# Mamba scan stage of a four-layer convolution network: side jobs carried from block to block, fixed buffers for them, shorter holds of their PSUM banks, sums copied out a few steps later, a quarter of du times B multiplied by diagonal matmuls

## The chip, the cores and the metric

The kernel runs on one core of a Trainium2 chip. A core has five engines that each execute their own instruction list in order: TensorE (PE in the profile; its weight loads are listed apart as PEld), VectorE (DVE), ScalarE (ACT), GpSimd (POOL) and SyncE (SP), which here only issues DMAs. They wait for one another through semaphores. The metric is the device time of one execution in microseconds. Before the change it is 17602.43 us, the median of three executions (17602.12 to 17605.28).

## The reference, cut to what matters

Four layers follow one another on a batch of 8 images of 256 channels and 32 x 32 pixels: an attention block with a feed-forward part, a second attention block, a quantised bottleneck, and a Mamba layer. The change lies in the Mamba layer alone. It reads each image in four directions (rows or columns first, forward or backward), runs the same Mamba on each sequence of L = 1024 tokens, and adds the four results:

```python
def _selective_scan(u, dt, A, Bm, Cm):          # d = 512 channels, n = 16 states
    def step(h, inp):
        u_t, dt_t, B_t, C_t = inp
        dA = jnp.exp(dt_t[:, :, None] * A)
        h = h * dA + dt_t[:, :, None] * B_t[:, None, :] * u_t[:, :, None]
        y = jnp.einsum('bdn,bn->bd', h, C_t)
        return (h, y)
    ...
def _mamba(u, W_in, conv_w, conv_b, W_x, W_dt, b_dt, A_log, D, W_out):
    x, z = jnp.split(u @ W_in.T, 2, axis=-1)
    x = silu(causal depthwise conv of 4 taps of x)           # cut
    x_dbl = x @ W_x.T
    dt = jax.nn.softplus(x_dbl[..., :16] @ W_dt.T + b_dt)
    Bm, Cm = x_dbl[..., 16:32], x_dbl[..., 32:]
    y = _selective_scan(x, dt, -jnp.exp(A_log), Bm, Cm) + x * D
    return (y * jax.nn.silu(z)) @ W_out.T
```

Everything is float32.

## The kernel before

The first phase computes layers one to three and leaves codes of the images in HBM. The second phase is the Mamba layer. It works through 64 blocks: 8 images x 4 directions x 2 halves of 512 tokens. A block has 64 units: for each of the 16 states s, four chunks c of 128 channels. A unit is one scan of 128 channels x 512 tokens on VectorE. Its parts are recorded in this order, and each engine executes its own instructions in the order in which they are recorded (`tc.manual_schedule()`):

```python
    def scaled(u, t):       # du*B of state s for 128 tokens t: tokens on partitions, 512 channels
        o = dbp.tile([P, DI], F32, name="dbu", tag="dbu")
        src, b = d.duT[h * TH + t], d.bT[:, h * TH + t, s : s + 1]
        if t == TH - 1 and s % 2:
            nc.gpsimd.tensor_scalar(o, src, b, zero, ALU.mult, ALU.add)      # L951
        else:
            nc.scalar.activation(o, src, AF.Identity, scale=b)               # L953
    def turned(u):          # turns four 128x128 pieces of it: channels on partitions
        db = ps_d.tile([P, HALF], F32, name="db", tag="db")
        for t, o in enumerate(units["dbu", u - c]):
            nc.tensor.transpose(db[:, t * P : (t + 1) * P], o[:, c * P : (c + 1) * P], ident)   # L962
    def decay(u):           # exp(dt*A)
        nc.scalar.activation(da, d.dt[c, h], AF.Exp, scale=am[:, a : a + 1])  # L973
    def scan(u):            # h = h*dA + db; then, for two chunks at once, h*C
        nc.vector.tensor_tensor_scan(x[:, ::step], da[:, ::step], db[:, ::step], ..., ALU.mult, ALU.add)  # L985
        if c % 2:
            ...             # in a first half: the last column is kept as the state   (L993)
            nc.gpsimd.tensor_tensor(pair, pair, cb.unsqueeze(1).to_broadcast([P, 2, HALF]), ALU.mult)     # L994
    def summed(u):          # adds h*C over the states in PSUM, turned back to tokens on partitions
        for t in range(TH):
            nc.tensor.matmul(banks[t][:, c * P : (c + 1) * P], lhsT=pair[:, c % 2, t * P : (t + 1) * P],
                             rhs=ident, is_transpose=True, ...)               # L1016
        ...                 # in four units of a block also x*D by a diagonal matmul  (L1024)
        if r == PER - 1 and n % 4 != 1:
            ...             # the four sums are copied out of PSUM (or added to yT)   (L1034-1038)

    for u in range(total):              # total = 64 blocks x 64 units, PER = 64
        n, r = divmod(u, PER)
        if r == LAG:                    # LAG = 4
            must, more = side(n)        # the side jobs that later blocks need
            jobs.add(0, must)
            jobs.add(1, more)
        scan(u)
        turned(u + 2)
        decay(u + AHEAD)                # AHEAD = 5
        ...                             # C rows (DMA), scaled() for two states ahead
        summed(u - LAG)
        jobs.step(0.85, 1)              # one step of the side jobs, with 0.85 matmuls and 1 activation of budget
        if r == PER - 8:
            jobs.drain([0])             # all jobs of the first queue are run to their end here
```

The side jobs prepare the next blocks: the input projection (`inputs`, L686), the 4-tap convolution as diagonal matmuls with silu and x_dbl (`mixed`, L738 to L780), dt and du (`steps`, L795 to L832), and they finish earlier ones (`fold`, `outputs`). Each is a Python generator; every `yield` ends its part in one step. At most four of the first queue run at a time; they share two PSUM banks, two sets of temporaries and two z tiles, which they count. A dt job before:

```python
            nc.scalar.activation(t, ps, AF.Abs)              # ps: its PSUM bank
            nc.scalar.activation(t, t, AF.Exp, scale=-1.0)
            nc.scalar.activation(o, t, AF.Ln, bias=1.0)
            nc.vector.tensor_scalar(u1, t, 1.0, -1.0, ALU.add, ALU.add)     # L810
            ...                                              # two steps later
            nc.gpsimd.tensor_tensor(t, t, u1, ALU.subtract)  # L812
            nc.gpsimd.tensor_tensor(o, o, t, ALU.add)        # L813
            ...                                              # four steps later
            nc.vector.scalar_tensor_tensor(o, ps, 0.0, o, ALU.max, ALU.add) # L815: still needs ps
            ...
            nc.gpsimd.tensor_tensor(u1, o, d.xs[c, h], ALU.mult)            # L818
            jobs.give("bank")
            ...                                              # turned by TensorE (L828), copied to duT (L832)
```

Of the kernel before, what the change touches and what calls it, by code (L numbers as in the profile page):

```python
# [547 lines left out]
class _Jobs:  # L548
# [14 lines left out]
    def take(self, what):  # L563
        while not self.room[what]:
            yield
        self.room[what] -= 1

    def give(self, what):
        self.room[what] += 1

    def step(self, pe, act):
        for k, v in (("pe", pe), ("act", act)):
            self.turns[k] = min(self.turns[k] + v, max(v, 1.0))
        for (wait, run), n in zip(self.queues, (4, 2)):
            while wait and len(run) < n:
                run.append(wait.pop(0))
            for j in list(run):
                try:
                    next(j)
                except StopIteration:  # L580
                    run.remove(j)
# [7 lines left out]
def phase_b(ctx, tc, i, col, ident, codes, out):  # L589
# [11 lines left out]
    dbp = ctx.enter_context(tc.tile_pool(name="db", bufs=2 * TH + 1))  # L601
    dap = ctx.enter_context(tc.tile_pool(name="da", bufs=6))
    hp = ctx.enter_context(tc.tile_pool(name="h", bufs=4))
    cbp = ctx.enter_context(tc.tile_pool(name="cb", bufs=3))
    tp = ctx.enter_context(tc.tile_pool(name="tp", bufs=4))
    zp = ctx.enter_context(tc.tile_pool(name="z", bufs=2))
# [5 lines left out]
    ps_p = ctx.enter_context(tc.tile_pool(name="ps_p", bufs=2, space=PSUM))  # L612
# [35 lines left out]
    jobs = _Jobs(bank=2, tmp=2, z=2)  # L648

    def pp():  # L650
        return ps_p.tile([P, HALF], F32, name="pp", tag="pp")

    def tmp():
        return tp.tile([P, HALF], F32, name="tmp", tag="tmp")

    def ztile():
        return zp.tile([P, HALF], F32, name="z", tag="z")
# [9 lines left out]
    def load_x(b, swap, h, box):  # L667

        cd = cdp.tile([P, CC, N], U8, name="cd", tag="cd")
        nc.sync.dma_start(cd, codes[b].rearrange("k p n -> p k n"))  # L670
        yield from lag(3)
        xf = cdp.tile([P, CC, HALF], F32, name="xf", tag="xf")
        for k in range(CC):
            yield from jobs.turn("act")
            if swap:
                v = cd[:, k].rearrange("p (a b) -> p b a", b=WW)[:, 16 * h : 16 * h + 16]
                nc.scalar.activation(xf[:, k].rearrange("p (a b) -> p a b", b=WW), v, AF.Identity, scale=col("s3"))
            else:
                nc.scalar.activation(xf[:, k], cd[:, k, hs(h)], AF.Identity, scale=col("s3"))
        yield  # L680
        box.append(xf)

    def project(xf, m0, ps):
        for k in range(CC):
            yield from jobs.turn("pe")
            nc.tensor.matmul(ps, lhsT=w_in[:, k, m0 : m0 + P], rhs=xf[:, k], start=(k == 0), stop=(k == CC - 1))  # L686
        yield from lag(2)

    def free():
        yield  # L690
        jobs.give("bank")

    def inputs(b, swap, xi, before=lambda: True):

        for h in range(2):
            box = []

            def first(h=h, box=box):
                while not before():
                    yield  # L700
                yield from load_x(b, swap, h, box)

            yield first()
            for c in range(DC):

                def one(h=h, c=c, box=box):
                    while not box:
                        yield
                    yield from jobs.take("bank")
                    ps = pp()  # L710
                    yield from project(box[0], c * P, ps)
                    if h == 0:
                        t = xip.tile([P, N + 2 * PAD], F32, name="xi", tag="xi")
                        nc.gpsimd.memset(t[:, :PAD], 0.0)
                        nc.gpsimd.memset(t[:, PAD + N :], 0.0)
                        xi[c] = t
                    nc.vector.tensor_copy(xi[c][:, PAD + h * HALF : PAD + (h + 1) * HALF], ps)
                    xi["done"] = xi.get("done", 0) + 1
                    yield from free()

                yield one()


    def mixed(n):
# [5 lines left out]
        def conv(c):  # L730
            while xi.get("done", 0) < 2 * DC:
                yield
            yield from jobs.take("bank")
            ps = pp()
            for k in range(4):
                yield from jobs.turn("pe")
                o = PAD + h * HALF + (PAD - k if d.back else k - PAD)
                nc.tensor.matmul(  # L738
                    ps, lhsT=cvd[:, 4 * c + k, :], rhs=xi[c][:, o : o + HALF], start=(k == 0), stop=(k == 3)
                )  # L740
            yield from lag(2)
            yield from jobs.turn("act")
            t = xsp.tile([P, HALF], F32, name="xs", tag="xs")
            nc.scalar.activation(t, ps, AF.Identity, bias=col("cv_b", c))  # L744
            d.xs[c, h] = t
            done.add(c)
            yield from free()
# [10 lines left out]
        def xdbl():  # L758
# [3 lines left out]
            yield from jobs.take("bank")  # L762
            ps = pp()
# [10 lines left out]
            yield from free()  # L774
            yield from jobs.take("bank")
            pt = pp()
# [4 lines left out]
            yield from free()  # L781
# [3 lines left out]
    def steps(n):  # L785
# [4 lines left out]
        def dt(c):  # L790
            yield from jobs.take("tmp")
            yield from jobs.take("bank")
            ps = pp()
# [8 lines left out]
            t = tmp()  # L802
            nc.scalar.activation(t, ps, AF.Abs)
            yield from jobs.turn("act")
            nc.scalar.activation(t, t, AF.Exp, scale=-1.0)
            yield from jobs.turn("act")
            o = dtp.tile([P, HALF], F32, name="dt", tag="dt")
            nc.scalar.activation(o, t, AF.Ln, bias=1.0)
            u1 = tmp()
            nc.vector.tensor_scalar(u1, t, 1.0, -1.0, ALU.add, ALU.add)  # L810
            yield from lag(2)
            nc.gpsimd.tensor_tensor(t, t, u1, ALU.subtract)  # L812
            nc.gpsimd.tensor_tensor(o, o, t, ALU.add)  # L813
            yield from lag(4)
            nc.vector.scalar_tensor_tensor(o, ps, 0.0, o, ALU.max, ALU.add)  # L815
            d.dt[c, h] = o
            yield from lag(1)
            nc.gpsimd.tensor_tensor(u1, o, d.xs[c, h], ALU.mult)  # L818
            jobs.give("bank")
# [4 lines left out]
            yield from jobs.take("bank")  # L824
            pt = pp()
# [4 lines left out]
            jobs.give("tmp")  # L830
            for t in range(TH):
                nc.vector.tensor_copy(d.duT[h * TH + t][:, c * P : (c + 1) * P], pt[:, t * P : (t + 1) * P])  # L832
            yield from free()
# [4 lines left out]
    def fold(swap, h):  # L838


        def one(c):
            yield from jobs.take("bank")
            ps = pp()
# [9 lines left out]
            yield from free()  # L853
# [3 lines left out]
    def outputs(b, h):  # L857
        box, done = [], set()

        def gate(c):  # L860
            while not box:
                yield
            yield from jobs.take("z")
            yield from jobs.take("bank")
            ps = pp()
            yield from project(box[0], DI + c * P, ps)

            t = ztile()
            nc.vector.tensor_scalar(t, ps, -44.0, None, ALU.max)
            yield from lag(2)  # L870
# [4 lines left out]
            nc.vector.tensor_tensor(t, ps, t, ALU.mult)  # L875
            yield from free()
            y = ys[c][:, hs(h)]
# [3 lines left out]
            jobs.give("z")  # L881

        def o3(cc):
# [3 lines left out]
            yield from jobs.take("z")  # L887
            yield from jobs.take("bank")
            ps = pp()
# [8 lines left out]
            o = ztile()  # L898
            nc.scalar.copy(o, ps)
            nc.sync.dma_start(out[b, cc * P : (cc + 1) * P, hs(h)], o)  # L900
            yield from free()
            jobs.give("z")
# [40 lines left out]
    def scaled(u, t):  # L943

        if u >= total:
            return
        n, d, h, s, _ = at(u)
        o = dbp.tile([P, DI], F32, name="dbu", tag="dbu")
        src, b = d.duT[h * TH + t], d.bT[:, h * TH + t, s : s + 1]
        if t == TH - 1 and s % 2:  # L950
            nc.gpsimd.tensor_scalar(o, src, b, zero, ALU.mult, ALU.add)  # L951
        else:
            nc.scalar.activation(o, src, AF.Identity, scale=b)  # L953
        units.setdefault(("dbu", u), []).append(o)

    def turned(u):
# [4 lines left out]
        for t, o in enumerate(units["dbu", u - c]):  # L961
            nc.tensor.transpose(db[:, t * P : (t + 1) * P], o[:, c * P : (c + 1) * P], ident)  # L962
# [43 lines left out]
    def summed(u):  # L1006
# [23 lines left out]
        if r == PER - 1 and n % 4 != 1:  # L1030
            for t in range(TH):
                o = yT[:, h * TH + t, :]
                if n % 4 == 3:
                    nc.vector.tensor_tensor(o, banks[t], o, ALU.add)  # L1034
                elif t % 2:
                    nc.vector.tensor_copy(o, banks[t])
                else:
                    nc.scalar.copy(o, banks[t])
# [6 lines left out]
    for t in range(TH):  # L1045
        scaled(DC, t)
# [3 lines left out]
    for u in range(total):  # L1050
        n, r = divmod(u, PER)
        if r == LAG:
# [4 lines left out]
        scan(u)  # L1057
        turned(u + 2)
# [3 lines left out]
        if c >= 1:  # L1062
            scaled(u - c + 2 * DC, c - 1)
        if c == DC - 1:
            scaled(u - c + 2 * DC, c)
        summed(u - LAG)
        jobs.step(0.85, 1)
        if r == PER - 8:
            jobs.drain([0])
    for u in range(total, total + LAG):  # L1070
        summed(u - LAG)
    jobs.add(0, fold(True, 0) + outputs(B - 1, 0) + outputs(B - 1, 1))
# [119 lines left out]
```

## Time and profile before

The trace covers one execution of 17602.1 us. The Mamba blocks begin with the first scan at 9475 us and end with the last at 17545 us.

| stretch | us | PE busy | DVE busy | ACT busy | POOL busy |
|---|---|---|---|---|---|
| layers one to three and set-up | 9475 | 8380 | 2362 | 2018 | 486 |
| 64 Mamba blocks | 8070 | 6678 | 5833 | 5985 | 6399 |
| last sums and outputs | 57 | 41 | 18 | 18 | 14 |

A busy share is an average over a stretch with different limits inside. TensorE's ends are modelled, so that a busy PE is not a PE at its peak: matmuls that follow one another overlap in the records, and the distance from start to start tells what one really costs. A float32 matmul stands in the records as two of the same shape, a transpose as one. In the rows of groups the columns are line, engine, operation, output<-inputs, shapes and count; then busy us and mean ns of one; then the idle time of the engine before them with what ended most of it. "issue" there means that no wait was seen to end.

### The profile page before, as it was taken

The numbers are of one execution on the slowest core, as the hardware profiler recorded it, in microseconds if no ns is written. First come the engines' busy times: TensorE is split into PE (matmuls) and PEld (weight loads), VectorE is DVE, ScalarE is ACT, GpSimd is POOL, SyncE is SP. The second block draws the span as 40 slices with busy tenths as digits, with TensorE's granted clock in tenths as the row PEclk, the third lists the DMA queues.
The fourth block names the chain that finished last, engine by engine and source line by source line (L and its number), as shares of the span: only waits on it lengthen the run. The fifth ranks groups of instructions, "written<-read, shape, count | busy, mean of one in ns | idle before, by whom it ended". The sixth has DMA issues, their size and how long they took to land. (4 is left out here: it accounts for less than half of the span.)

```text
span 17602.1 us, 170403 instructions
## 1 busy us (share of the span) xinstructions
PE 15098.7 (86%) x66144; PEld 10332.0 (59%) x66144; DVE 8213.0 (47%) x8852; ACT 8021.1 (46%) x12205; POOL 6899.4 (39%) x4689
## 2 busy tenths in 40 slices
PE   8988988979889889798897888888888888888888
PEld 5655655556556555565564665656666565666666
DVE  3123123131231231312314776767777776777777
ACT  2221222222222222222224777777777777777777
POOL 0001001010010010100104787878787787878778
PEclk6556556565565565655657999999999999999999
DMA  0000000000000000000000111111111111111111
GB/s 15 0 2 3 0 1 3 0 3 0 1 3 0 1 3 0 3 0 1 0 0 23 35 37 37 36 36 37 37 36 37 37 36 37 36 37 36 35 38 38
DMA packets 177335, 319.06 MB, mean 18 GB/s; under 512 B 20417, under 2 KB 37185, under 8 KB 176530
## 3 DMA queue, kind: packets, MB, share of 16 engines
q1 hardware_dynamic: 176530, 308.17, 5.7%
q8 instruction: 524, 8.59, 0.2%
q14 instruction: 281, 2.30, 0.0%
HBM read 295.51 MB, written 12.58 MB: 18 GB/s over the span
## 5 line engine op out<-in xcount | busy, mean ns | idle before, releaser
L994 POOL TENSOR_TENSOR h<-h,cb 128x1024 f32<-128x1024 f32 x2048 | 4834.0, 2369 | 945.5 <-issue 407.8
L962 PE MATMUL db<-ident,dbu 128*128 128x128 f32 x16384 | 2769.9, 293 | 895.8 <-DVE h L985 720.0
L973 ACT ACTIVATE da<-dt,am 128x512 f32<-128x512 f32 x4096 | 2899.4, 714 | 911.7 <-DVE h L985 896.6
L305 DVE TENSOR_REDUCE mx<-p 128x1 f32<-128x1024 f32 x768 | 940.6, 1225 | 5034.8 <-PE p L300 5034.8
L314 PEld LDWEIGHTS p<-t,t 128*128 128x128 f32 x12288 | 2576.1, 318 | 1100.9 <-issue 1037.0
L312 ACT COPY t<-pt 128x1024 f32<-128x1024 f32 x768 | 777.2, 1012 | 5102.3 <-PE pt L310 5102.3
L962 PEld LDWEIGHTS db<-ident,dbu 128*128 128x128 f32 x16384 | 2005.8, 149 | 1817.2 <-issue 835.7
L1016 PE MATMUL py<-ident,h 128*128 128x128 f32 x16384 | 2656.0, 288 | 253.0 <-POOL h L994 250.4
L300 PE MATMUL p<-t,t 32*128 32x512 f32 x3072 | 2781.0, 1055 | 0.0
L314 PE MATMUL p<-t,t 128*128 128x32 f32 (+1 forms) x12288 | 2686.0, 398 | 18.0 <-ACT t L312 18.0
L953 ACT ACTIVATE dbu<-duT,bT 128x512 f32<-128x512 f32 x3584 | 2496.9, 710 | 318.2 <-PE db L962 314.3
L985 DVE TENSOR_TENSOR_SCAN h<-da,st,db 128x512 f32<-128x512 f32 x2048 | 2504.6, 1265 | 283.9 <-PE db L962 263.6
L985 DVE TENSOR_TENSOR_SCAN h<-da,db 128x512 f32<-128x512 f32 x2048 | 2385.6, 1205 | 391.0 <-PE db L962 361.0
L1016 PEld LDWEIGHTS py<-ident,h 128*128 128x128 f32 x16384 | 2062.2, 149 | 333.1 <-POOL h L994 329.9
L274 POOL TENSOR_SCALAR t<-t,ga,gs 128x1024 f32<-128x1024 f32 x32 | 37.9, 1195 | 5170.3 <-DVE gs L271 5170.3
L310 PE MATMUL pt<-ident,t 128*128 128x128 f32 x6144 | 1473.6, 418 | 110.5 <-ACT t L307 105.8
L300 PEld LDWEIGHTS p<-t,t 32*128 32x128 f32 x3072 | 839.9, 306 | 956.2 <-issue 938.5
L310 PEld LDWEIGHTS pt<-ident,t 128*128 128x128 f32 x6144 | 1312.6, 241 | 138.6 <-ACT t L307 107.3
L381 POOL TENSOR_TENSOR t<-t,t 128x1024 f32<-128x1024 f32 x16 | 37.1, 2336 | 3143.9 <-ACT t L378 3143.9
L738 PE MATMUL pp<-xi,cvd 128*128 128x512 f32 x2048 | 997.2, 607 | 5.8 <-ACT xs L744 5.4
L307 ACT ACTIVATE t<-p,mx 128x1024 f32<-128x1024 f32 x768 | 860.0, 1120 | 281.2 <-DVE mx L305 281.2
L342 DVE SCALAR_TENSOR_TENSOR t<-t,cols,t 128x961 f32<-128x961 f32 (+1 forms) x512 | 617.0, 1273 | 1.1
(176 smaller groups left out, 11064.8 us busy)
## 6 DMA issues: line engine op xcount, KB each, us to landing
cb<-c_d SPq DMA_DIRECT2D x1024, 256.0 KB, 3.2
cd<-codes SPq DMA_DIRECT2D x48, 256.0 KB, 3.6
t<-in_x_dram SPq DMA_DIRECT2D x8, 1024.0 KB, 5.0
out_dram<-z SPq DMA_DIRECT2D x32, 256.0 KB, 2.0
codes<-cd SPq DMA_DIRECT2D x16, 128.0 KB, 1.7
c_d<-xd SPq DMA_DIRECT2D x64, 32.0 KB, 1.6
w_pi<-in_w_pi_dram SPq DMA_DIRECT2D x1, 1024.0 KB, 8.5
w_in<-in_w_in_dram SPq DMA_DIRECT2D x1, 1024.0 KB, 4.9
```

What stands on the lines that cost most here:

```text
L300: nc.tensor.matmul(s[:, j : j + HALF], lhsT=q(h)[:, t * P : (t + 1) * P], rhs=k(h)[:, j : j + HALF], start=True, stop=True,)
L305: nc.vector.tensor_reduce(mx, s, AX.X, ALU.max, negate=True)
L307: nc.scalar.activation(e, s, AF.Exp, bias=mx, accum_out=rsum[:, h : h + 1])
L310: nc.tensor.transpose(pt[:, j, :], e[:, j * P : (j + 1) * P], ident)
L314: nc.tensor.matmul(po[:, h * hd : (h + 1) * hd], lhsT=et[:, j, :], rhs=vt[:, j, h * hd : (h + 1) * hd], start=(j == 0), stop=(j == NT - 1),)
L738: nc.tensor.matmul(ps, lhsT=cvd[:, 4 * c + k, :], rhs=xi[c][:, o : o + HALF], start=(k == 0), stop=(k == 3))
L953: nc.scalar.activation(o, src, AF.Identity, scale=b)
L962: nc.tensor.transpose(db[:, t * P : (t + 1) * P], o[:, c * P : (c + 1) * P], ident)
L973: nc.scalar.activation(da, d.dt[c, h], AF.Exp, scale=am[:, a : a + 1])
L985: nc.vector.tensor_tensor_scan(x[:, ::step], da[:, ::step], db[:, ::step], 0.0 if first else d.st[:, a : a + 1], ALU.mult, ALU.add)
L994: nc.gpsimd.tensor_tensor(pair, pair, cb.unsqueeze(1).to_broadcast([P, 2, HALF]), ALU.mult)
L1016: nc.tensor.matmul(banks[t][:, c * P : (c + 1) * P], lhsT=pair[:, c % 2, t * P : (t + 1) * P], rhs=ident, is_transpose=True, start=(s == 0 ...
```

## The change

1. Side jobs may be left over. The full drain at unit 56 of every block goes; in its place the recording runs job steps only until the four du tiles of the next block are there. Jobs that are not needed yet go on in the next block. Five jobs of the first queue may run at a time instead of four, and a step has 0.8 matmuls of budget instead of 0.85. In the last two blocks nothing is left to do there.
2. Buffers of side jobs are fixed by number (`pp0`, `pp1`, `tmp0` to `tmp3`, `z0`, `z1`) and handed round in a list. This, with a token for the image tile (`xf`) and a flag that x_dbl is there, keeps jobs of two blocks apart.
3. PSUM banks are held for less time: dt reads its bank with VectorE right after the first exponential and frees it; the gate multiplies y by z straight from PSUM and frees the bank before its three activations.
4. The block's sums are copied out of PSUM one unit later, after the scan of unit 4 of the next block instead of at the end of unit 3.
5. Of the four 128-token pieces of `du*B`, the last is no longer scaled (by GpSimd or ScalarE) and then transposed. GpSimd makes a 128x128 diagonal of B (`dg`), and TensorE multiplies the unscaled duT by it, which scales and turns at once. `da` gets 7 buffers instead of 6, `dbu` 7 instead of 9, `dg` 3.

The number of the other instructions stays. The diff, cut to its core:

```diff
-        for (wait, run), n in zip(self.queues, (4, 2)):
+        for (wait, run), n in zip(self.queues, (5, 2)):
...
-    dbp = ctx.enter_context(tc.tile_pool(name="db", bufs=2 * TH + 1))
-    dap = ctx.enter_context(tc.tile_pool(name="da", bufs=6))
+    dbp = ctx.enter_context(tc.tile_pool(name="db", bufs=2 * TH - 1))
+    dgp = ctx.enter_context(tc.tile_pool(name="dg", bufs=3))
+    dap = ctx.enter_context(tc.tile_pool(name="da", bufs=7))
...
-    jobs = _Jobs(bank=2, tmp=2, z=2)
+    jobs = _Jobs(bank=[0, 1], tmp=[0, 1], z=[0, 1], xf=[0])
...                                   # in steps(), a dt job
+            while "xd" not in d.done[h]:
+                yield
...
-            t = tmp()
+            t, u1 = tmp(2 * kt), tmp(2 * kt + 1)
             nc.scalar.activation(t, ps, AF.Abs)
+            nc.scalar.activation(t, t, AF.Exp, scale=-1.0)
+            yield from lag(1)
+            o = dtp.tile([P, HALF], F32, name="dt", tag="dt")
+            nc.vector.scalar_tensor_tensor(o, ps, 0.0, t, ALU.max, ALU.add)
+            nc.vector.tensor_scalar(u1, t, 1.0, -1.0, ALU.add, ALU.add)
+            yield from free(kb)
+            yield
             yield from jobs.turn("act")
-            nc.scalar.activation(t, t, AF.Exp, scale=-1.0)
-            ...
-            nc.gpsimd.tensor_tensor(t, t, u1, ALU.subtract)
+            nc.scalar.activation(t, t, AF.Ln, bias=1.0)
+            nc.gpsimd.tensor_tensor(o, o, u1, ALU.subtract)
+            yield
             nc.gpsimd.tensor_tensor(o, o, t, ALU.add)
-            yield from lag(4)
-            nc.vector.scalar_tensor_tensor(o, ps, 0.0, o, ALU.max, ALU.add)
...                                   # scaled() and turned()
-        if t == TH - 1 and s % 2:
-            nc.gpsimd.tensor_scalar(o, src, b, zero, ALU.mult, ALU.add)
-        else:
-            nc.scalar.activation(o, src, AF.Identity, scale=b)
+        if t == TH - 1:
+            o = dgp.tile([P, P], F32, name="dg", tag="dg")
+            nc.gpsimd.tensor_scalar(o, ident, b, zero, ALU.mult, ALU.add)
+            units.setdefault(("dbu", u), []).append((src, o))
+            return
+        o = dbp.tile([P, DI], F32, name="dbu", tag="dbu")
+        nc.scalar.activation(o, src, AF.Identity, scale=b)
...
-            nc.tensor.transpose(db[:, t * P : (t + 1) * P], o[:, c * P : (c + 1) * P], ident)
+            nc.tensor.matmul(
+                db[:, t * P : (t + 1) * P], lhsT=o[:, c * P : (c + 1) * P], rhs=m, is_transpose=m is ident,
+                start=True, stop=True,
+            )
...                                   # the loop over units
-        if r == LAG:
+        if r == LAG + 1:
...
         scan(u)
+        if r == LAG:
+            close(n - 1)              # the sums are copied out here
...
-        jobs.step(0.85, 1)
-        if r == PER - 8:
-            jobs.drain([0])
+        jobs.step(0.8, 1)
+        if r == PER - 8 and n + 1 < len(blocks):
+            e, h = blocks[n + 1]
+            while not {("du", c) for c in range(DC)} <= e.done[h]:
+                jobs.step(1, 1)
```

The change is meant to keep the scan running while side jobs are worked off, and to take scaling work from ScalarE.

## The prediction

> **What bounds the kernel now.** I read the page first: busy shares, then the 40 slices, then the costliest groups. The chain of work that ended last is of no help here; its shares add up to some 5% of the span, because it breaks off soon. The slices show two kernels in one. Until slice 22 GpSimd is almost idle and the TensorE clock is granted at 0.5 to 0.6; after it every engine is busy. The change touches only the second part, so I asked for busy time by stretch: layers one to three, the Mamba blocks, the end.
>
> ```profile
> POOL 0001001010010010100104787878787787878778
> PEclk6556556565565565655657999999999999999999
> ...
> 0.00:9475.00 9475.00, 8380.00 (x25592) 5357.41 (x25592) 2362.03 (x2678) 2017.91 (x2715) 485.83 (x166) 0.58 0.01 2
> 9475.00:17545.00 8070.00, 6677.82 (x40450) 4956.15 (x40451) 5832.97 (x6150) 5984.92 (x9461) 6399.18 (x4514) 0.93 0.12 37
> ```
>
> The columns of the last two lines are the stretch, its length, then busy us of PE, PEld, DVE, ACT and POOL, the granted clock, DMA share and GB/s. So 9475 us stay as they are and 8070 us, 126.1 us for each of 64 blocks, are in play. POOL is busy 6399/64 = 100.0 us of a block, DVE 91.1, ACT 93.5. PE's 104.3 is modelled; its own cost comes from start-to-start distances below. No engine is full, so I looked at one block (the 26th, 12645 to 12777 us) on the timelines of DVE and POOL, where unit 56 ends and the drain begins:
>
> ```profile
> 12734.87 2.45 DVE L985 TENSOR_TENSOR_SCAN h<-da,st,db 128x512 f32<-128x512 f32 x2 [0.15 <-PE db L962]
> 12752.91 0.69 DVE L717 COPY xi<-pp 128x512 f32<-128x512 f32 x1 [15.59 <-PE pp L686]
> ...
> 12768.46 8.30 DVE L985 TENSOR_TENSOR_SCAN h<-da,st,db 128x512 f32<-128x512 f32 x7
> ```
>
> ```profile
> 12769.87 9.40 POOL L994 TENSOR_TENSOR h<-h,cb 128x1024 f32<-128x1024 f32 x4 [25.84 <-issue]
> ```
>
> No scan starts for 31 us, while side jobs alone run; then seven scans go at full pace, 1.15 us each. POOL waits 25.8 us, listed as "issue", yet it ends with the first scans after the drain. Over blocks 8 to 55 of the trace (count from 0) the hole between the 57th and 58th scan is 23.4 us, and such a block takes 127.6 us. POOL idles 27.1 us in it: with the hole and the refill after it this is nearly all of its idle time. Outside, POOL is all but full: 22.1 us of its idle time is booked on instructions after the hole, but some 18 of them end within a few us of it. So between drains GpSimd sets the pace, and the drain is what keeps a block 26 us above GpSimd's own work.
>
> The groups that the sums below use, from the page and from POOL's groups in the set-up stretch (9000 to 9475 us):
>
> ```profile
> L994 POOL TENSOR_TENSOR h<-h,cb 128x1024 f32<-128x1024 f32 x2048 | 4834.0, 2369 | 945.5 <-issue 407.8
> L962 PE MATMUL db<-ident,dbu 128*128 128x128 f32 x16384 | 2769.9, 293 | 895.8 <-DVE h L985 720.0
> L1016 PE MATMUL py<-ident,h 128*128 128x128 f32 x16384 | 2656.0, 288 | 253.0 <-POOL h L994 250.4
> L738 PE MATMUL pp<-xi,cvd 128*128 128x512 f32 x2048 | 997.2, 607 | 5.8 <-ACT xs L744 5.4
> ```
>
> ```profile
> L274 POOL TENSOR_SCALAR t<-t,ga,gs 128x1024 f32<-128x1024 f32 x2 | 2.4, 1194 | 613.8 <-DVE gs L271 613.8
> L638 POOL TENSOR_SCALAR dd<-ident,cols 128x128 f32<-128x128 f32 x4 | 2.3, 602 | 0.0
> L951 POOL TENSOR_SCALAR dbu<-duT,bT,zero 128x512 f32<-128x512 f32 x1 | 0.8, 762 | 2.2 <-DVE duT L832 2.2
> ```
>
> L994 alone is 32 x 2.37 = 75.8 us of a block. L962 and L1016 wait for DVE and for POOL: TensorE is not the first bound yet.
>
> **What the Trainium skill says.** "TensorE: Matmul & The Clock Gate" (Terms) gives the transpose mode as four times faster for float32. "FP8 and Floating Point Precision" (TensorE Precision Notes) says that true float32 takes four passes. The trace agrees on the second and not on the first: a float32 matmul of 128 columns (L1024) stands as two records whose starts are 111 ns apart, 222 ns together; a transpose (L962, L1016) is one record, 109 ns from start to start. So transposing is twice as fast, and the measured 109 and 222 are used. "Perfetto Trace Analysis" (Tensor Engine Instruction) says that the profile's end of a matmul is estimated, which is why I use starts: 293 ns "mean" against 109. The same page (Optimization Strategy) reads consistent bubbles on the engine that should be saturated as a hint at too few buffers. Here the repeated bubble on POOL has another cause, the recorded order: side jobs stand between two scans.
>
> **The change part by part.**
>
> *The drain.* I compared the order of instructions of both programs between the 57th and 58th scan of each block. Before, the eight blocks of an image hold 23, 27, 19, 14, 14, 27, 11 and 14 side matmuls of 512 columns there, 149 in all. After, 14, 3, 24, 7, 1, 0, 14 and 1, which is 64. Two of eight blocks keep a long hole (the third, with four of the gates' projections, two whole dt chains and silu; and the seventh), three or four lose it. Scaled by matmuls the mean hole becomes 23.4 x 64/149 = 10.0 us. Estimated by chains (ACT's silu with its two table loads of 1.28 us, dt's path through PE, ACT, DVE, POOL, PE, DVE of some 9 us) I get 11, 3.5, 20, 5, 2, 0.5, 14 and 2, mean 7.3. I take 9. The work that leaves the hole does not vanish: (149 - 64)/8 = 10.6 matmuls of 2 x 0.43 us (L738 and L686 start 429 to 432 ns apart, two records each) = 9.1 us of PE move among the units of each block.
>
> *du times B.* POOL loses 8 x 0.803 = 6.4 us (L951 over all blocks) and gains 16 diagonals. What does one cost? L951 and L274, both of two operations, give (1194 - 762)/512 = 0.84 ns a column, so some 440 ns at 128 columns; L638, of one operation, took 602 at 128. Start to start that is 0.36 to 0.58. I take 0.40: 6.4 us, so POOL stays at 100 us (103 at worst). ACT loses 8 x 0.71 (L953) = 5.7 us. PE turns 64 transposes a block into matmuls: 64 x (222 - 109) = 7.2 us more.
>
> *Where this puts PE.* Its cost before, by starts: L962 and L1016 256 x 0.109 each = 55.8; L738 32 x 0.43 = 13.8; L686 4.8; L795 4.3; L766 3.4; L1024 3.6; the rest 4.7: 90 us of 126. After: 97 us at full clock, as much as POOL. The clock was granted at 0.93 in this part, which asks for 104 us if it stays.
>
> *Shorter holds.* In blocks 8 to 55 DVE waits 3.6 us a block at L815 for POOL (L813). That goes, since the new form needs only ACT. But DVE is not the bound: its scans wait 9.9 us a block for PE (L962) outside the hole, and POOL is full meanwhile. I count nothing for it. The later copy of the sums moves a wait of under 1 us (L1036 and L1034) and costs nothing either. The fixed numbers change no amount of buffers. The same holds for `da` with 7.
>
> *Sum.* A block is POOL's work plus POOL's idle time. Work 100. Idle: 26.1 x 9/23.4 = 10. A third term is what two nearly full engines cost each other, PE at 97 and POOL at 100 with two db banks and four h pairs between them. From nothing in the trace can I work this out; now 13% of the time in the blocks runs at half clock, and PE's extra 16 us between scans (9.1 + 7.2) meet a slack of 18 us of PE waits there. My guess is 6 us. Together 116 us, 10.1 less than 126.1; 64 blocks: 646 us. 17602 - 646 = 16956, put at 16950.
>
> **Rivals.**
>
> *TensorE becomes the bound.* For: 97 us by starts, 104 at the granted clock, and it works in order, so that a side matmul of 0.86 us in front of a db group delays a scan of 1.15 us; 16 us more per block between scans. Against: it idled 17.9 us a block outside the holes, mostly waiting for scans (11.9), and a denser PE may be granted more clock. If it binds at 0.93 with the hole of 9 us counting half: 104 + 4.5 + waits of 12 = 120 to 122 us, 17210 to 17340.
>
> *GpSimd alone binds and the holes close for good.* For: blocks of few side matmuls (fifth, sixth, eighth) leave nothing in the hole. Against: the third keeps 24. It would give 100 + 5 = 105 to 108 us, 16250 to 16450.
>
> *The hole is hidden anyway, and the work only moves.* If units between drains were as full on every engine as GpSimd's share suggests, moving 9 us of PE work and POOL's dt work into them lengthens them by as much as the hole shrinks. For: POOL's 4.1 us in the hole move as well. Against: the other engines have 10 to 35 us to spare a block. It would leave 124 to 127 us, 17450 to 17650. Slower than before it gets only if dg (needed two units after it is recorded, three before) stalls PE at every state: 16 stalls of 1 us would eat the gain, and twice that would turn it.
>
> **Range and chances.** The middle comes from 116 us a block; 110.5 (holes at 7 us, 2 us of mutual waits) gives 16600, and 122 (TensorE) gives 17340. The range 16600 to 17340 should hold 8 in 10. Over 2% faster is below 17250, that is under 120.6 us a block: 0.77. Within 2%: 0.18. Slower: 0.05.
>
> **What would show it.** Right: stretch one unchanged at 9475; holes between 57th and 58th scan of 5 to 12 us, long ones in the third and seventh block of an image; POOL busy near 6400 us, in blocks of 116 us a share of 86%; db matmuls with dg as two records of 111 ns; dg near 0.4 us. Wrong: dg at 0.6 or more; POOL's idle time spread over the units, ended by DVE scans that wait for PE (TensorE is then the bound); blocks outside the holes longer than their old 104 us by more than 5.

## The result and the profile after

The changed kernel takes 16966.1 us (median of four runs, 16959.9 to 16968.9), against 17602.3 for the kernel before: a ratio of 0.9638 with a 95% interval of 0.9621 to 0.9655. That is 636 us less; the prediction had said 16950.

Busy time by stretch, again with the stretch, its length, busy us of PE, PEld, DVE, ACT and POOL, granted clock, DMA share and GB/s:

```profile
0.00:9475.00 9475.00, 8377.98 (x25604) 5357.99 (x25604) 2363.46 (x2681) 2019.68 (x2721) 487.06 (x169) 0.58 0.01 2
9475.00:16910.00 7435.00, 6734.98 (x44541) 5220.98 (x44540) 5805.65 (x6148) 5635.58 (x8943) 6459.70 (x5024) 0.97 0.13 40
```

The first stretch did not move, and the blocks shrank from 8070 to 7435 us. GpSimd has nearly the same work, 6460 us or 100.9 a block (100.0 before), ScalarE 350 us less, and TensorE was granted 0.97 of its clock instead of 0.93. Over blocks 8 to 55 (counted from 0) a block takes 117.5 us instead of 127.6. The hole between its 57th and 58th scan is 10.4 us instead of 23.4; everything else in the block takes 107.1 us instead of 104.2. So 13.0 us came from the hole and 2.9 were given back between scans.

The hole is not gone everywhere. By place in the image (eight blocks) it is 16.3, 3.6, 30.6, 9.6, 1.4, -0.1, 20.5 and 1.4 us (minus: the scans followed without a break). The first, third and seventh place keep a long one. VectorE's timeline at the end of block 26 (counted from 0), a third block of its image; columns as before: start, length, engine, line, operation, tiles, number, idle time before it and its releaser:

```profile
12583.43 1.22 DVE L1000 TENSOR_TENSOR_SCAN h<-da,db 128x512 f32<-128x512 f32 x1 [3.28 <-PE db L974]
12589.16 0.69 DVE L879 TENSOR_SCALAR z<-pp 128x512 f32<-128x512 f32 x1 [4.52 <-PE pp L688]
...
12595.52 0.69 DVE L817 SCALAR_TENSOR_TENSOR dt<-pp,tmp 128x512 f32<-128x512 f32 x1 [1.72 <-ACT tmp L814]
...
12611.00 0.69 DVE L879 TENSOR_SCALAR z<-pp 128x512 f32<-128x512 f32 x1 [12.79 <-PE pp L688]
...
12615.62 4.54 DVE L1000 TENSOR_TENSOR_SCAN h<-da,db 128x512 f32<-128x512 f32 x4
```

Gates (L879) and dt jobs (L817) run there while no scan does, as their place in the recorded order says.

The groups of the changed parts, GpSimd's and then TensorE's; columns are busy us and mean ns of one, then idle time before with its releasers:

```profile
L961 POOL TENSOR_SCALAR dg<-ident,bT,zero 128x128 f32<-128x128 f32 x1022 | 474.2, 464 | 0.0
```

```profile
L974 PE MATMUL db<-ident,dbu 128*128 128x128 f32 x12276 | 2131.0, 283 | 287.8 <-DVE h L1000 259.9 <-ACT dbu L965 14.0 <-ACT tmp L813 7.2
L974 PE MATMUL db<-dg,duT 128*128 128x128 f32 x8185 | 1641.5, 283 | 304.0 <-POOL dg L961 302.9
```

The 4096 diagonal matmuls stand as 8192 records, 111 to 112 ns from start to start; 109 for a transpose. From the start of a diagonal to the start of GpSimd's next operation it takes 0.39 to 0.41 us in most cases, where nothing else delays that one.

The waits have turned round. The rows give who waited for whom, us in total, times and the longest, over the blocks; first before, then after:

```profile
PE db L962 <- DVE h L985: 720.0, 613, 3.5
...
DVE h L985 <- PE db L962: 624.6, 926, 3.4
...
DVE dt L815 <- POOL dt L813: 223.0, 122, 2.7
...
PE db L962 <- POOL dbu L951: 132.7, 165, 1.9
```

```profile
DVE h L1000 <- PE db L974: 982.1, 1176, 5.5
ACT dbu L965 <- PE db L974: 886.5, 658, 4.0
...
PE db L974 <- POOL dg L961: 302.9, 144, 5.2
...
PE db L974 <- DVE h L1000: 259.9, 280, 2.8
```

Where a row ends with "DVE h" the engine named first waited for a scan. Before, TensorE waited for scans more than scans for TensorE. Now scans wait 982 us for TensorE, and TensorE waits 260 for scans, 4.1 us a block instead of 11.3: most of its slack has gone. On top of that it stands 303 us before a diagonal matmul until GpSimd has made the diagonal. VectorE's wait for GpSimd in dt (223 us) has gone.

### The profile page after: what moved, and what is told of

Same layout as the page of the kernel before. It is cut to its first block, busy times and chain, and to the rows that moved or that the text cites. A ratio compares the mean times of both kernels' runs of the same rounds, so it can differ in the third digit from the quotient of the medians.

```text
span 16962.4 us, 178465 instructions
## 1 busy us (share of the span) xinstructions
PE 15151.2 (89%) x70240; PEld 10596.2 (62%) x70240; DVE 8186.1 (48%) x8852; ACT 7673.5 (45%) x11693; POOL 6960.1 (41%) x5201
## 5 line engine op out<-in xcount | busy, mean ns | idle before, releaser
L1009 POOL TENSOR_TENSOR h<-h,cb 128x1024 f32<-128x1024 f32 x2048 | 4840.3, 2368 | 444.1 <-DVE h L1000 152.9
L988 ACT ACTIVATE da<-dt,am 128x512 f32<-128x512 f32 x4096 | 2829.7, 710 | 205.7 <-DVE h L1000 200.9
L965 ACT ACTIVATE dbu<-duT,bT 128x512 f32<-128x512 f32 x3072 | 2185.5, 712 | 935.4 <-PE db L974 886.5
L1031 PE MATMUL py<-ident,h 128*128 128x128 f32 x16384 | 2542.4, 278 | 68.9 <-POOL h L1009 52.6
L974 PE MATMUL db<-ident,dbu 128*128 128x128 f32 x12288 | 2134.3, 283 | 291.1 <-DVE h L1000 262.5
L974 PEld LDWEIGHTS db<-ident,dbu 128*128 128x128 f32 x12288 | 1480.6, 144 | 1417.4 <-issue 643.6
L1031 PEld LDWEIGHTS py<-ident,h 128*128 128x128 f32 x16384 | 1984.9, 145 | 96.6 <-POOL h L1009 67.5
L974 PE MATMUL db<-dg,duT 128*128 128x128 f32 x8192 | 1643.2, 283 | 304.0 <-POOL dg L961 302.9
L974 PEld LDWEIGHTS db<-dg,duT 128*128 128x128 f32 x8192 | 1277.0, 197 | 345.4 <-POOL dg L961 345.2
L745 PE MATMUL pp<-xi,cvd 128*128 128x512 f32 x2048 | 1055.3, 620 | 14.6 <-DVE dt L817 14.6
```

What stands on the lines that cost most here:

```text
L745: nc.tensor.matmul(ps, lhsT=cvd[:, 4 * c + k, :], rhs=xi[c][:, o : o + HALF], start=(k == 0), stop=(k == 3))
L974: nc.tensor.matmul(db[:, t * P : (t + 1) * P], lhsT=o[:, c * P : (c + 1) * P], rhs=m, is_transpose=m is ident, start=True, stop=True,)
```

## The experiments

All times are medians of four runs (three rounds and the profiled one); "hole" and "rest" are means of blocks 8 to 55 of the profiled run, in us, and their sum is a block. The last column is the interval of the ratio to the kernel before, from the same chip.

| kernel | us | hole | rest | ratio, 95% |
|---|---|---|---|---|
| before | 17602 | 23.4 | 104.2 | |
| changed | 16966 | 10.4 | 107.1 | 0.962 to 0.966 |
| no diagonal matmuls | 16850 | 11.7 | 104.1 | 0.956 to 0.959 |
| drain put back | 17286 | 15.1 | 107.9 | 0.980 to 0.984 |
| before, with diagonal matmuls | 17872 | 23.4 | 108.6 | 1.014 to 1.017 |
| long holds | 17123 | 18.0 | 102.0 | 0.971 to 0.974 |
| diagonals made by ScalarE | 16789 | 11.1 | 103.7 | 0.952 to 0.955 |
| one addition of dt on VectorE | 17155 | 9.6 | 110.8 | 0.973 to 0.976 |
| even budget | 16900 | 1.9 | 114.4 | 0.959 to 0.962 |
| sums copied early | 16967 | 10.6 | 106.9 | 0.963 to 0.966 |
| even budget, no diagonals | 16614 | 1.8 | 109.9 | 0.943 to 0.945 |
| even budget, diagonals by ScalarE | 16747 | 2.1 | 111.9 | 0.950 to 0.953 |
| even budget, no diagonals, all scaling on ScalarE | 16587 | 1.9 | 109.4 | 0.941 to 0.944 |
| before, all scaling on ScalarE | 17421 | 23.4 | 101.5 | 0.988 to 0.992 |

The theory at the start: the gain is the shorter hole; GpSimd's work sets the pace between holes; the diagonals cost TensorE little. The rivals: TensorE is the bound; ScalarE's relief is part of the gain; only leaving the drain counts.

**No diagonal matmuls** (the changed kernel with the old scaling and transposes):

```diff
-        if t == TH - 1:
-            o = dgp.tile([P, P], F32, name="dg", tag="dg")
-            nc.gpsimd.tensor_scalar(o, ident, b, zero, ALU.mult, ALU.add)
-            units.setdefault(("dbu", u), []).append((src, o)); return
+        if t == TH - 1 and s % 2:
+            nc.gpsimd.tensor_scalar(o, src, b, zero, ALU.mult, ALU.add)
+        else:
+            nc.scalar.activation(o, src, AF.Identity, scale=b)
```

> The changed kernel with its fifth part undone: all four pieces of du*B are scaled on ScalarE or GpSimd and transposed, as before (da again 6 buffers, for room); everything else as changed. My theory: the gain is that of the holes, POOL keeps its 101 us of work a block, and PE is freed of 7.2 us, which eases the waits of scans for db but is not the bound: 114 to 117 us a block, 16750 to 16950. Rival 'TensorE binds': all of the 7.2 us comes back, 110 us, about 16500. Rival 'ScalarE's relief was part of the gain' (5.7 us fewer on ACT): slower than the changed kernel, 17050 to 17300.

It is 116 us faster than the changed kernel. The fifth part as a whole is a loss: whatever its relief of ScalarE (350 us) is worth, the rest of it costs more. (The edit also puts the numbers of `dbu` and `da` buffers back, here as in the runs below without diagonals.) But the 460 us of matmuls that go do not come back in full either, so TensorE alone is not the bound. The hole grew by 1.3 us and the rest fell by 3.0.

**Before, with diagonal matmuls alone** (the same edit the other way round, on the kernel before):

> The kernel before with the fifth part alone: a quarter of du*B by diagonal matmuls. The drain, its 149 side matmuls and long holds stay. My theory: POOL sets the pace between drains and its work does not change, PE has room there: 17600 to 17700, the same or a little slower. Rival 'ScalarE's relief helps': 17200 to 17500. Rival 'TensorE binds': 64 x 7.2 = 460 us more, 18050.

It is 271 us slower than before, more than the theory's 100 at most. The hole is the same; the rest grew by 4.4 us a block. The scans' waits for db rose from 625 to 911 us, and TensorE waited 263 us for dg, where it had waited 133 for GpSimd's scaled piece:

```profile
DVE h L992 <- PE db L966: 910.7, 1061, 3.7
...
PE db L966 <- POOL dg L953: 262.6, 260, 1.8
```

So even with a slack of TensorE in the profile the fifth part delays scans. How much of it is the matmuls and how much the wait for dg, this run does not tell.

**Drain put back** (the changed kernel with `jobs.drain([0])` at unit 56):

```diff
-        if r == PER - 8 and n + 1 < len(blocks):
-            e, h = blocks[n + 1]
-            while not {("du", c) for c in range(DC)} <= e.done[h]:
-                jobs.step(1, 1)
+        if r == PER - 8:
+            jobs.drain([0])
```

> The changed kernel with the full drain at unit 56 put back; short holds, fixed buffers and diagonal matmuls stay. In its recorded order the hole of eight blocks holds 88 side matmuls of 512 columns (before the change 149, changed 64). My theory, by matmuls: holes of 23.4 x 88/149 = 14 us instead of the 10.4 measured in the changed kernel, 3.5 us a block, 17150 to 17250. Rival 'leaving the drain is the whole gain': back to 17550 to 17700. Rival 'the hole is hidden anyway': 16950 to 17000.

It is 320 us slower: near the theory, a little above its range, and not all of the gain. The hole of 15.1 us stands against 13.8 from the count of its matmuls.

**Long holds** (dt and gate hold their bank as before):

```diff
-            nc.vector.scalar_tensor_tensor(o, ps, 0.0, t, ALU.max, ALU.add)
-            nc.vector.tensor_scalar(u1, t, 1.0, -1.0, ALU.add, ALU.add)
-            yield from free(kb)
...
+            nc.gpsimd.tensor_tensor(t, t, u1, ALU.subtract)
+            nc.gpsimd.tensor_tensor(o, o, t, ALU.add)
+            yield from lag(4)
+            nc.vector.scalar_tensor_tensor(o, ps, 0.0, o, ALU.max, ALU.add)
...
+            nc.gpsimd.tensor_tensor(u1, o, d.xs[c, h], ALU.mult)
+            jobs.give("bank", kb)
```

> The changed kernel with its third part undone: a dt job and a gate keep their PSUM bank as long as before (dt until GpSimd has made du, the gate over its three activations), and the order of operations in a dt job is that of before. The hole then holds 86 side matmuls of 512 columns (64 in the changed kernel), in twice as many steps. My theory: longer holes, 15 to 18 us against 10.4, and VectorE waits again for GpSimd in dt: 5 to 9 us a block, 17280 to 17550. Rival 'the holds are a detail, the drain is what counts': 16950 to 17050.

It is 157 us slower, so the holds count, if for half of the least that the theory gave them. The hole is 18.0 us as expected; the rest is 5.1 us shorter, probably because more of the side work sits in the hole (86 matmuls of an image instead of 64). Against the kernel with all of the old scheme and diagonals (17872), short holds without leaving the drain are worth 586 us, leaving it with long holds 749, both together 906: each takes work out of the same hole. (These two also carry the fixed buffers, the fifth slot, the later copy and the seventh `da`.)

**Diagonals made by ScalarE:**

```diff
-            nc.gpsimd.tensor_scalar(o, ident, b, zero, ALU.mult, ALU.add)
+            nc.scalar.activation(o, ident, AF.Identity, scale=b)
```

> The changed kernel, but ScalarE makes the 128x128 diagonal dg (scale by B) instead of GpSimd: POOL loses 16 x 0.46 us a block, ScalarE gains some 16 x 0.3. The run without the fifth part was 116 us faster than the changed kernel. Theory 'that loss is dg's wait': TensorE stands 4.7 us a block in front of a db matmul until POOL has made dg; with dg on ScalarE the wait goes, and the fifth part's loss with it: 16780 to 16880. Rival 'the loss is TensorE's 7.2 us more of matmuls': 16930 to 17000. If POOL's work sets the pace, 7 us less of it gives more than either: 16550 to 16700.

177 us faster than the changed kernel, and even faster than without diagonals. TensorE's wait for the diagonal fell from 303 to 38 us:

```profile
PE db L974 <- ACT dg L961: 37.6, 40, 2.4
```

The rest is 103.7 us instead of 107.1. GpSimd also lost 6.7 us of work a block (6460 to 6029 us in all); were GpSimd's work the pace, that alone should have given more (16550 to 16700). A block became only 2.7 us shorter, for work and wait together, and the two are not told apart. So the wait for dg is the likely cause of most of the fifth part's loss, but it is not shown: this kernel also spares GpSimd 5.8 us a block against the one without diagonals, and that relief may hide what the 7.2 us of matmuls cost. A kernel with the holes, no diagonals and all scaling on ScalarE would decide it; it was not run. (With the holes closed this comparison exists, see below.)

**One addition of dt on VectorE:**

```diff
-            nc.gpsimd.tensor_tensor(o, o, t, ALU.add)
+            nc.vector.tensor_tensor(o, o, t, ALU.add)
```

> The changed kernel with one of the three GpSimd operations of a dt job (the addition of the logarithm) on VectorE: POOL 4 x 1.28 = 5.1 us a block less, VectorE some 4 x 0.6 = 2.4 more. Theory 'POOL's work plus its idle time is the block': 3 to 5 us a block, 16640 to 16780. Rival 'TensorE or the waits of scans for db set the pace': 16920 to 17020.

GpSimd has 3.7 us less work a block (6222 us in all), and the kernel is 189 us slower: the theory falls. The waits over the blocks point at VectorE's list:

```profile
PE db L974 <- DVE h L1000: 702.5, 452, 4.8
DVE h L1000 <- PE db L974: 593.1, 905, 2.2
...
POOL h L1009 <- DVE h L1000: 459.8, 448, 9.4
...
DVE dt L825 <- POOL dt L823: 391.8, 156, 4.1
```

The addition (L825) stands in VectorE's list between two scans and waits there 392 us for GpSimd's subtraction; the others then wait for the scan: TensorE 703 us instead of 260, GpSimd 460 instead of 153. The addition itself takes 1.44 us there, not the 0.6 assumed, 363 us in all. Work was taken from the fullest engine, and as much work and an in-order wait were put on the engine that feeds it; which of these two costs the 189 us is not told apart.

**Even budget.** A step's allowance of matmuls was capped at 1. With 0.8 (or 0.85, as before) added to nothing it takes two steps to reach 1, and what is over is cut: one side matmul in every second unit, not 0.8 a unit. So 0.85 and 0.8 let in the same matmuls. The edit keeps the remainder and sets 0.7:

```diff
-            self.turns[k] = min(self.turns[k] + v, max(v, 1.0))
+            self.turns[k] = min(self.turns[k] + v, max(v, 1.0) + (v < 1) * 0.99)
...
-        jobs.step(0.8, 1)
+        jobs.step(0.7, 1)
```

> The changed kernel with an even budget: the allowance of 0.8 matmuls a unit was capped at 1, so that in fact one side matmul is let in every second unit; now 0.7 a unit, not lost. In the recorded order the hole of eight blocks then holds 14 side matmuls of 512 columns instead of 64, the job steps there go from 87 to 13. Theory: holes of about 2 us instead of 10.4, the work moves among the units; POOL at 101 us of work: 109 to 113 us a block, 16450 to 16700. Rival 'TensorE binds, the work only moves': 16900 to 17050.

The hole closes to 1.9 us as foreseen, but the kernel gains 66 us only, as the rival had it: the rest grows by 7.3 us. TensorE's timeline in block 26 shows how a unit looks with a side matmul and without:

```profile
12500.99 1.02 PE L688 MATMUL pp<-xf,w_in 128*128 128x512 f32 x2
12501.85 0.49 PE L974 MATMUL db<-ident,dbu 128*128 128x128 f32 x3
12502.18 0.39 PE L974 MATMUL db<-dg,duT 128*128 128x128 f32 x2
12502.41 0.60 PE L1031 MATMUL py<-ident,h 128*128 128x128 f32 x4
12502.84 1.02 PE L688 MATMUL pp<-xf,w_in 128*128 128x512 f32 x2
12503.70 0.49 PE L974 MATMUL db<-ident,dbu 128*128 128x128 f32 x3
12504.03 0.39 PE L974 MATMUL db<-dg,duT 128*128 128x128 f32 x2
12504.25 0.60 PE L1031 MATMUL py<-ident,h 128*128 128x128 f32 x4
12504.69 0.49 PE L974 MATMUL db<-ident,dbu 128*128 128x128 f32 x3
```

No wait stands in any of these rows. From one side matmul to the next there are 1.85 us (12500.99 to 12502.84); the unit without one takes 0.99 (12503.70 to 12504.69). A scan takes 1.15. In these rows TensorE sets the pace of a unit with a side matmul, and over the blocks the scans' waits for db rose from 982 to 1199 us:

```profile
DVE h L1000 <- PE db L974: 1198.8, 1369, 7.5
```

**Even budget without diagonals, and with ScalarE's** (both edits together):

> Even budget (0.7 side matmuls a unit, not lost) and no diagonal matmuls: the even budget alone closed the holes from 10.4 to 1.9 us but gave 66 us only, since the units outside became 7.4 us a block longer. Theory 'TensorE's slack between the scans is used up': without the diagonals TensorE has 7.2 us a block more of it, so most of the hole of 11.7 us that the kernel without diagonals still has comes back: 16350 to 16600, against 16850 with the holes. Rival 'the work moved into the units costs what it costs, in VectorE's order': again some 66 us, 16750 to 16830.

> Even budget, and ScalarE makes the diagonals. TensorE keeps its 7.2 us of extra matmuls but not the 4.7 us a block that it stood before them waiting for GpSimd. Theory 'TensorE's slack': part of the hole of 11 us comes back, 16500 to 16680, against 16789 with the holes. Rival 'costs what it costs': 16700 to 16790.

Without diagonals closing the hole gives 237 us (16850 to 16614, 14 us short of the expected range), where it gave 66 with them. That fits the theory that TensorE then has slack for the moved matmuls. Yet even here, of the 10.0 us by which the hole shrank only 4.2 stay; the other 5.8 lengthen the rest. With the diagonals on ScalarE closing the hole gives 41 us, as the rival had it: with TensorE's wait for GpSimd gone and its matmuls still there, nearly all of the moved work shows. With the hole closed the fifth part costs 286 us (16900 against 16614), of which ScalarE's diagonals save 153.

**The same, all scaling on ScalarE:**

```diff
-        if t == TH - 1 and s % 2:
-            nc.gpsimd.tensor_scalar(o, src, b, zero, ALU.mult, ALU.add)
-        else:
-            nc.scalar.activation(o, src, AF.Identity, scale=b)
+        nc.scalar.activation(o, src, AF.Identity, scale=b)
```

> As the even budget without diagonals, but ScalarE scales all four pieces of du*B in every state; GpSimd loses 8 x 0.8 = 6.4 us a block, ScalarE gains 5.7 and with some 99 us is as full as GpSimd was. Theory: GpSimd's work does not set the pace, what counts is the wait of TensorE for GpSimd's piece (2.3 us a block without diagonals): 0 to 150 us faster than with GpSimd's share. Rival 'GpSimd's work sets the pace': 350 us faster. Rival 'ScalarE is now the bound': slower.

27 us faster; at 16587 us it is the fastest kernel of the study, 379 us below the changed one. GpSimd's work fell by 5.9 us a block, TensorE's wait for GpSimd's piece (2.5 us a block) went, and a block became 0.4 shorter. But ScalarE got 4.4 us more, which may have eaten a gain. Busy time over the blocks (columns as above; last ScalarE 6228, GpSimd 6016):

```profile
9475.00:16541.00 7066.00, 6381.88 (x40452) 4706.51 (x40451) 5908.39 (x6148) 6228.49 (x9967) 6016.30 (x4003) 0.96 0.14 42
```

This kernel is also the fair counterpart of the even budget with ScalarE's diagonals: holes closed (1.9 and 2.1 us), GpSimd with the same work (6016 and 6017 us), TensorE waiting for a piece or a diagonal from GpSimd in neither. The diagonals cost 160 us there (16747 against 16587), 2.5 us a block for 7.2 us of matmuls, although ScalarE has 5.1 us less to do. So with the holes closed the fifth part costs time without GpSimd's diagonals, too.

**Before, all scaling on ScalarE:**

> The kernel before the change with one thing different: ScalarE scales all pieces of du*B, GpSimd none. POOL loses 8 x 0.8 = 6.4 us a block, ScalarE gains 5.7. The prediction read the profile as 'between drains GpSimd sets the pace': then a block falls by about 6 us outside its hole, 17200 to 17300. Theory after the other runs: every engine waits for every other through short buffers, no engine's work sets the pace by itself: 17500 to 17620. Rival 'ScalarE becomes the bound', slower than 17650.

182 us faster than before: 2.8 us a block for 6.1 us of GpSimd's work, between both theories. The 2.1 us a block that TensorE had waited for GpSimd's piece went too, so how much of the 2.8 is the work and how much the wait is not told apart.

**Sums copied early** (the fourth part undone; the side jobs start one unit earlier). The job steps shift by a unit here, and the first copies of the next image's sums into `ys` get ahead of the last matmuls of the output projection that read `ys`; it computes with other values there, with the same work.

> The changed kernel with its fourth part undone: the sums are copied out at the end of unit 3, as before, instead of after the scan of unit 4, and the side jobs are added one unit earlier. Theory: a wait of about 1 us a block comes back on VectorE in front of the copies: 16960 to 17040. Rival 'it matters for the scans': over 17100.

No difference to the changed kernel, although the wait came back as expected: VectorE stands 92 us (1.4 us a block) before these copies until TensorE has summed, 1 us in the changed kernel. Meanwhile the scans' waits for db fell from 982 to 909 us. The fourth part is worth nothing measurable; a wait can be removed and the time stay.

## Why the prediction was right, step by step

**The hole.** 9 us were predicted and 10.4 measured. Of its two ways to get there the count of matmuls in the recorded order was the better: scaled block by block (23.4 us for 149/8 matmuls) it gives 17.6, 3.8, 30.2, 8.8, 1.3, 0, 17.6 and 1.3, within 3 us of every measured value. It also has the first place as long as the seventh (14 matmuls each), which the prediction's words, "the third" and "the seventh", pass over: 16.3 us were measured there. For the even budget it says 2.2 (measured 1.9), for the drain 13.8 (15.1). The estimate by chains had the long ones a third too short. With long holds the count fails (13.5 against 18.0), probably because chains of waits and not matmuls fill that hole.

**The diagonals.** Costs were as said: 222 to 224 ns against 109, a diagonal at 0.40 us predicted and 0.39 to 0.41 measured, GpSimd at 100.9 us of work. What they do to the time was left inside a guess of 6 us for mutual waits. It is measured now: 1.8 us a block (116 us) in the changed kernel, 4.2 in the kernel before. The wait for dg, which the prediction named as what could turn the gain, is 4.7 us a block; in the kernel without it (ScalarE's diagonals) the loss is gone as long as the holes stay, with GpSimd's load lower as well. The four passes of a float32 matmul, which the prediction quotes, no run here shows: the trace has two records to a matmul and no matmul of another type to compare. Against a transpose it shows a factor of two.

**Shorter holds.** "I count nothing for it" was wrong in part. Taking VectorE's wait for GpSimd was named and did happen (223 us to none), but the holds also decide how many side jobs get done before unit 56: 157 us. The count of 64 matmuls had it in, booked as the drain's.

**What sets the pace between holes.** The sum, 100 of work, 10 of hole and 6 of waits, is an account: GpSimd's work plus its idle time is always the block, and 100.9 + 15.3 is what came out. That its total hit is partly luck. Over blocks 8 to 55 GpSimd idles 16.1 us a block, but 7.0 of it in the hole and the 8 us behind it, and 9.1 elsewhere, where 10 and 6 were said: one term too high and one too low, by 3 us each. The second was called a guess.

The reading behind it, "between drains GpSimd sets the pace", failed. Before the change, too, 5.9 of GpSimd's 27.2 us of idle time lay outside the hole and the 8 us behind it. Six us of its work less gave 0.4 us; in the kernel before 2.8, with a wait removed as well; 3.7 less work with a new wait and new work in VectorE's list made a block 3 us longer. And with the holes closed GpSimd still idles 15.0 us a block (even budget), or 11.3 without diagonals. Each of these runs loads another engine with what GpSimd loses, so they show that its work alone is not the pace, not that it is worth nothing.

What the rows bear out is the other sentence, that 16 us of extra TensorE work "meet a slack of 18 us of PE waits there": most of the slack was used up, and the rest grew by 2.9 us. After that the third rival, that the work only moves, comes true: the next 8.5 us of hole bought 1.2. "TensorE becomes the bound" named the engine that the scans came to wait for, but 17210 to 17340 was too dark for the changed kernel. TensorE's granted clock rose from 0.93 to 0.97, which that rival had left at 0.93. What raised it stays open: TensorE's busy share in the blocks, by its modelled ends, rose from 83% to 91%, but in the first stretch it is 88% at a granted clock of 0.58.

What stays open: how much of the rest, 109 us in the fastest kernel where ScalarE, the fullest engine by measured ends, is busy 97 us of a whole block, comes from db's two banks and how much from the order. A third bank would have to come from the side jobs' two, and might lengthen their holes; it was not tried.

## What to carry to other kernels

When one engine's order mixes a critical stream with side work, count what the recorded order puts into the stalled stretch: the count of its dominant operation can scale the stall well before anything runs; where chains of waits fill it, as with long holds here, it falls short. A high busy share and waits that point at an engine do not make it the bound; take a few us of its work away without adding a wait or as much work elsewhere, and see. Work that is moved out of a stall is free only as long as the engine that takes it has slack between the critical operations; after that the stall just changes its place, and what was bought with that engine's time (here the diagonals) turns into a loss.

## What the runs showed of the hardware that was not expected

VectorE's `tensor_scalar` of 128 x 512 (L818, both operands in SBUF) took from 0.41 to 2.8 us in the changed kernel, with a median of 1.1. In the hole shown above, with GpSimd idle, it took 0.42; between scans a few us before, with GpSimd at its multiplications (L1009), 2.47:

```profile
12566.88 2.47 DVE L818 TENSOR_SCALAR tmp<-tmp 128x512 f32<-128x512 f32 x1
...
12596.13 0.42 DVE L818 TENSOR_SCALAR tmp<-tmp 128x512 f32<-128x512 f32 x1
...
12597.79 0.42 DVE L818 TENSOR_SCALAR tmp<-tmp 128x512 f32<-128x512 f32 x1
```

Of the 256, all 31 during which GpSimd was idle took 0.42 us; the 159 that ran mostly beside a multiplication of GpSimd's (L1009) had a median of 1.26. But a busy GpSimd does not always lengthen it: the last row overlaps two operations of GpSimd (L823 and L887),

```profile
12597.85 1.48 POOL L887 TENSOR_TENSOR ys<-ys,z 128x512 f32<-128x512 f32 x1
```

and beside a diagonal (L961) the median of 18 is 0.43. That it waits for GpSimd's access to the same memory is an inference: "GPSIMD Engine Reference" (Specifications) of the Trainium skill says that GpSimd's SBUF interfaces are shared with VectorE, with contention for VectorE instructions that use two ports or read two SBUF inputs. L818 reads one tensor; whether it runs in a mode of two ports, no run here shows, and none varied it. At four a block it may be worth 3 us (an estimate: four times 1.1 less 0.42).

And a `tensor_scalar` of GpSimd on 128 x 128 took 0.60 us with one operation (L638) but 0.45 with two (L961); why is not shown.
